# A graph-network kernel's first stage: loading x at once and placing the adjacency check between the layernorms

## The chip, the cores and the metric

The kernel runs on one core of a Trainium2 chip. The metric is the device time of one execution in microseconds (us); a run's time is compared by the median of several executions. The engines are called by the profile's names: PE (TensorE, matrix products), DVE (VectorE), ACT (ScalarE), POOL (GpSimd) and SP (SyncE, which here only issues transfers). A line number such as L391 is a line of the kernel's source; the profile prints it with each instruction.

## The reference, cut to what matters

Four graph layers, each of the form `x = x + layer(relu(layernorm(x)), adj)`, work on x of 8 x 2048 x 64 (batch, node, feature) and one adjacency matrix adj of 2048 x 2048. The first layer is a hypergraph attention, the second a Chebyshev convolution, the third repeats a product with adj three times, the fourth is an attention over neighbours.

```python
def _layernorm(x, axis=-1, eps=1e-5):
    m = jnp.mean(x, axis=axis, keepdims=True)
    v = jnp.var(x, axis=axis, keepdims=True)
    return (x - m) / jnp.sqrt(v + eps)
...
    h = jnp.maximum(_layernorm(x, axis=-1), 0.0)
    x = x + _L0_gnn_ref(h, L0_gnn_H, adj, 64, L0_gnn_W, ...)
...
        h = x @ W          # in _L0_gnn_ref: the "features" of the first layer
        deg = jnp.maximum(adj.sum(-1), 1.0)[:, None]
```

The case is about what the kernel does ahead of the first layer's attention: the first layernorm and relu, the product with W, and a reading of the whole of adj, by which it counts each node's neighbours and decides whether the matrix is sparse enough for its short way.

## The kernel before

**Layout.** x comes transposed, as 4 pairs of batches (`NP`) x 128 (two batches of 64 features, on the partitions) x 2048 nodes. The nodes are worked on in 4 chunks (`NC`) of 512 (`CW`). adj is read in 16 rows of tiles (`NT`), each 128 x 2048, 1 MB; below such a row of tiles is called a row.

**The first stage** is `start` (L629). It loops over the chunks. Each chunk is loaded by `load_x` (L262, into a buffer of two) and normalised by `norm_parts` (L284): for each of the four pairs PE makes a product with `center`, which takes the mean away (L290); ACT squares it (L291); the relu of it goes to `xr`, by turns on DVE (L294) and ACT (L296). PE adds up the squares (`to_rows`), ACT takes the root (L299), DVE its reciprocal (L300). Here the generator yields; `norm` runs it through. The second part spreads the reciprocals over the partitions on PE (`from_rows`) and DVE multiplies (L641), which gives `hn`, kept for the whole first layer in the memory q0 and q1.

`features` (L669) makes, for one chunk, h = hn W in two layouts: four products of 512 columns, copied by ACT to h_t (L676), and four node tiles of sixteen small products, copied by ACT to h_n (L682; memory q4 and q5). In the loop it follows one chunk behind the norms, and for the last chunk it comes after the check.

**The check** is `check_adj` (L368). For each of the 16 rows: SP loads it (L390) into one of four places; ACT squares it, which also adds up the degree (L391); DVE compares the square with the row, to see that all is 0 or 1 (L392); POOL sets the diagonal to zero (L395) and writes the result to `links` in DRAM (L399); PE makes thirteen small products `seen` of it. A place of the four is free for the next load when DVE has compared it, and a place of `squares` when POOL's write and PE's products are done. Then come a few small counts on DVE and PE (L406 to L423) that end in `flag`, a number by which all engines branch into one of two versions of the rest.

**What sets the order.** The tile framework collects the instructions of the program, puts them in an order for each engine by a priority and by its own idea of when each is ready, and adds the waits. An engine then works its instructions in that order and stands still at the first that has to wait. The check is written after the loop over the chunks, and the scheduler itself pulls the rows forward, between the norms. In the order that it builds, ACT squares two rows within and behind chunk 0's norm, then two or four rows at a time; SP issues the first two chunks, the first two rows, and the other two chunks later, when a buffer is free. All PSUM results of norms and features share six banks (`bank`), so a product waits for the reader of the result six places earlier.

`keep_in_program_order` (in `behind`, L193) marks an instruction that the scheduler must keep behind those marked or written ahead of it on its engine. The stage before doesn't use it.

Of the kernel before, what the change touches and what calls it, by code (L numbers as in the profile page):

```python
# [7 lines left out]
F = mybir.dt.float32  # L8
# [4 lines left out]
AF = mybir.ActivationFunctionType  # L13
OP = mybir.AluOpType
# [5 lines left out]
P = 128  # L20
# [3 lines left out]
NP = NB // 2  # L24
NT = N // P
R = P // NP
CW = 512
NC = N // CW
TC = CW // P
# [106 lines left out]
class Kernel:  # L136
# [39 lines left out]
    def mm(self, out, lhsT, rhs, start=True, stop=True):  # L176
        self.nc.tensor.matmul(out, lhsT, rhs, start=start, stop=stop)  # L177
# [102 lines left out]
    def norm(self, *args):  # L280
        for _ in self.norm_parts(*args):
            pass
# [85 lines left out]
    def check_adj(self, pool, slots, seen, ps, flag):  # L368


        nc, adj = self.nc, self.a["adj"]
        limit = self.limits(pool)
        over = pool.tile([P, limit.shape[1] + 2], F, name="over")
        ones = pool.tile([P, P], BF, name="ones")
        nc.vector.memset(ones, 1.0)
        rows = [slots.tile([P, 2, N], F, name=f"rows{i}", tag=f"q{6 + i}") for i in range(2)]
        squares = slots.tile([P, 4, N], BF, name="squares", tag="q8")
        same = pool.tile([P, NT], F, name="same")
        deg = pool.tile([P, NT], F, name="deg")
        own = pool.tile([P, NT], F, name="own")  # L380
        equal = pool.tile([P, N], BF, name="equal")
        one = pool.tile([P, 1], BF, name="one_bf")
        nc.vector.memset(one, 1.0)
        nc.sync.dma_start(
            own, bass.AP(tensor=adj.tensor, offset=adj.offset, ap=[[N + 1, P], [P * (N + 1), NT]])
        )
        for t in range(NT):
            row, sq = rows[t // 2 % 2][:, t % 2], squares[:, t % 4]
            here = slice(t * P, (t + 1) * P)
            nc.sync.dma_start(row, adj[here])  # L390
            nc.scalar.activation(sq, row, AF.Square, accum_out=deg[:, t : t + 1])  # L391
            nc.vector.scalar_tensor_tensor(  # L392
                equal, row, 1.0, sq, op0=OP.mult, op1=OP.is_equal, accum_out=same[:, t : t + 1],
            )
            nc.gpsimd.affine_select(  # L395
                out=sq[:, here], in_=sq[:, here], compare_op=OP.not_equal, fill=0.0, base=0,
                pattern=[[-1, P]], channel_multiplier=1,
            )
            nc.gpsimd.dma_start(self.links[here], sq)  # L399
            for i in range(FAR):  # L400
                c = (HUBS + i) * P
                self.mm(
                    seen[:, t, i : i + 1], sq[:, c : c + P], one,
                    start=t == 0 and i == 0, stop=t == NT - 1 and i == FAR - 1,
                )
        hm = slots.tile([P, NT, D], F, name="hm", tag="q9")  # L406
        nc.sync.dma_start(hm, self.a["H"].rearrange("(t p) e -> p t e", p=P))
        nc.vector.tensor_scalar(hm, hm, 0.0, None, op0=OP.is_gt)
        nc.vector.tensor_reduce(self.deg[:, 0], hm, axis=AX.X, op=OP.add)
        self.count_nodes(pool, ones, limit, over, 0, ps)  # L410
        nc.vector.tensor_sub(self.deg[:, 1], deg, own)
        self.count_nodes(pool, ones, limit, over, 1, ps)
        bad = pool.tile([P, 1], F, name="bad")
        nc.vector.tensor_reduce(bad, same, axis=AX.X, op=OP.add)
        nc.vector.tensor_scalar(over[:, -2:-1], bad, float(N * NT), None, op0=OP.is_lt)
        nc.vector.tensor_scalar(self.edges, seen, 0.0, None, op0=OP.is_gt)
        self.count_lists(pool, ones, limit, over, ps)
        nc.vector.tensor_reduce(bad, over, axis=AX.X, op=OP.max)
        pt = ps.tile([P, CW], F, name="chain")[:1, :P]
        nc.tensor.transpose(pt, bad, self.ident)  # L420
        one = pool.tile([1, 1], F, name="one")
        nc.vector.tensor_reduce(one, pt, axis=AX.X, op=OP.max)
        nc.vector.tensor_scalar(flag, one, 0.0, None, op0=OP.is_gt)  # L423

        nc.vector.memset(self.self_weight, 0.0)
        alone = self.edges.rearrange("p t i -> p (t i)")[:, HUBS * FAR :: FAR + 1]
        weight = self.self_weight[:, HUBS:]
        nc.vector.tensor_scalar(weight, alone, -1.0, 1.0, op0=OP.mult, op1=OP.add)
        nc.vector.tensor_mul(weight, weight, own[:, HUBS:])
        nc.vector.tensor_scalar_max(deg, deg, 1.0)  # L430
        nc.vector.reciprocal(deg, deg)
        pr = ps.tile([P, CW], F, name="chain")[:NT, :P]
        nc.tensor.transpose(pr, deg, self.ident)
        rows = pool.tile([NT, P], F, name="rows")
        nc.vector.tensor_copy(rows, pr)
        nc.sync.dma_start(self.rdeg, rows)
# [192 lines left out]
    def start(self, pool, slots):  # L629

        nc, tc, a = self.nc, self.tc, self.a
        self.deg = pool.tile([P, 2, NT], F, name="deg")
        self.edges = pool.tile([P, NT, FAR], BF, name="edges")
        self.self_weight = pool.tile([P, NT], F, name="self_weight")
        flag = pool.tile([1, 1], I32, name="flag")
        with tc.tile_pool(reuse_waits="tile", name="k00", bufs=1) as k:
            ww = self.block_diag(k, a["W"], "ww")
            hn = Halves(slots, "hn", ("q0", "q1"), False)

            def write(q, ch, xr, scale):  # L640
                nc.vector.tensor_mul(hn(q)[:, ch * CW : (ch + 1) * CW], xr, scale)  # L641

            with (
                tc.tile_pool(reuse_waits="tile", name="links_ps", bufs=1, space=PSUM) as lps,
                tc.tile_pool(reuse_waits="tile", name="ln", bufs=2) as w,
                tc.tile_pool(reuse_waits="tile", name="ln_ps", bufs=6, space=PSUM) as ps,
            ):
                seen = lps.tile([P, NT, FAR], F, name="seen")
                self.h = (
                    hn, Halves(slots, "h_t", ("q2", "q3"), False),  # L650
                    Halves(slots, "h_n", ("q4", "q5"), True),
                )

                def bank():
                    return ps.tile([P, CW], F, name="bank")

                for ch in range(NC):
                    x = self.load_x(w, 0, ch)
                    xr = w.tile([P, NP, CW], F, name="xr", bufs=1)
                    sq = w.tile([P, NP, CW], F, name="sq", bufs=1)  # L660
                    std = w.tile([P, CW], F, name="std", bufs=1)
                    self.norm(ch, x, xr, sq, std, bank, write)
                    if ch > 0:
                        self.features(ww, ch - 1, bank)
                self.check_adj(k, slots, seen, lps, flag)
                self.features(ww, NC - 1, bank)
        return flag

# [2618 lines left out]
```

## Time and profile before

| what | value |
|---|---|
| median of 3 runs (lowest, highest) | 1926.74 us (1921.63, 1930.95) |
| the profiled execution | 1917.82 us |
| its span in the profile | 1916.1 us, 22580 instructions |
| busy shares over the span: PE, DVE, POOL, ACT | 88%, 72%, 56%, 43% |
| flag ready (end of L423) | 96.05 us |
| last copy of the stage's features on ACT (L682) | ends 99.65 us |
| comparisons of rows on DVE (L392), 16 | 36.7 us busy |
| squares of rows on ACT (L391), 16 | 30.4 us busy |
| moved by DMA in the first 97 us | some 30 MB, at about 400 GB/s while it is full |

The busy shares are averages over stages of different kinds, and the chain of waits that the page gives begins only at 809 us, so it says nothing about the first stage. The stage has to be read from its own stretch, 0 to 97 us, which is 5% of the span: from the timeline (start, duration, engine, line, operation, output and input), from the waits of one engine in that stretch, and from a table of busy times by stretches. In such a table each engine's column holds its busy time and, in brackets, the number of its instructions; PEclk is the granted clock of PE as a share of the full one, "DMA share" the mean busy share of the 16 DMA engines.

### The profile page before, as it was taken

The page shows a single profiled execution, that of the slowest core. Times are in us where ns is not written, and L with a number is a line of the kernel's source. Part 1 is how long each engine was busy: PE and PEld are TensorE (multiplying, and loading weights), DVE is VectorE, ACT ScalarE, POOL GpSimd, SP SyncE. Part 2 cuts the span into 40 slices and gives each one's busy share as a digit, 9 for nine tenths or more (in the row PEclk, how much of TensorE's full clock was granted, in tenths as well). Part 3 has the DMA queues.
Part 4 walks back from the last instruction along what each step waited for, and adds up shares of the span by engine and source line. Part 5 has one row for each costly group of instructions (what it writes and reads, how often), then busy time and mean ns, then how long its engine had stood idle before and what let it go on. Part 6 is the DMA issues. An engine that isn't in the chain of part 4 may idle for free.

```text
span 1916.1 us, 22580 instructions
## 1 busy us (share of the span) xinstructions
PE 1682.1 (88%) x7139; PEld 959.6 (50%) x7139; DVE 1376.8 (72%) x2281; ACT 818.7 (43%) x1650; POOL 1078.3 (56%) x1039
## 2 busy tenths in 40 slices
PE   5888899998997788899999999889999999679885
PEld 2446766664333454344343435358777575345432
DVE  6887778884677878778888777557666676558874
ACT  5732544454666654222111010057676754466300
POOL 1101366776762755887687756547373641677760
PEclk8998999998998899999999989999999999789887
DMA  9741223334545774324142232168788774766655
GB/s 340 286 124 46 67 93 101 112 124 159 172 131 152 212 226 155 97 81 125 39 110 98 72 106 77 51 210 274 242 253 261 234 244 148 241 175 180 183 174 196
DMA packets 127372, 305.25 MB, mean 159 GB/s; under 512 B 29681, under 2 KB 33537, under 8 KB 122113
## 3 DMA queue, kind: packets, MB, share of 16 engines
q0 software_dynamic: 45328, 149.60, 26.7%
q1 hardware_dynamic: 79600, 149.82, 23.5%
q10 hardware_dynamic: 2304, 4.20, 0.6%
q8 instruction: 60, 0.98, 0.2%
q14 instruction: 80, 0.65, 0.1%
HBM read 240.41 MB, written 63.14 MB: 158 GB/s over the span
## 4 chain that ended last, share of the span: by engine, by line
PE 35%; DMA 7%; POOL 5%; DVE 5%; issue 4%; ACT 1%; SPq 0%; DVEq 0%; POOLq 0%; ACTq 0%
PE pk L177 17%; PE acc L177 11%; POOL ring L2976 3%; DMA raw<-sent,index 3%; PE bank L177 1%; PE pn L177 1%; DMA ring<-f_rows,near 1%; POOL raw L2646 1%; PE pw L177 1%; PE pz L1955 1%; PE side L177 1%; DMA q<-att_rows 1%; POOL half L1872 1%; PE first L177 1%; PE p L177 1%
## 5 line engine op out<-in xcount | busy, mean ns | idle before, releaser
L2646 POOL DMA_INDIRECT raw<-sent,index x300 | 314.0, 1047 | 286.1 <-DVE part_lo L2664 143.0
L2663 ACT CAST part_hi<-raw 128x512 fp32r<-128x512 f32 x352 | 211.3, 619 | 299.9 <-PE acc L177 202.1
L2664 DVE TENSOR_TENSOR part_lo<-raw,part_hi 128x512 fp32r<-128x512 f32 x352 | 263.6, 769 | 88.4 <-ACT part_hi L2663 80.5
L177 PE MATMUL pk<-q,w 128*128 128x512 f32 (+1 forms) x768 | 305.6, 613 | 5.4 <-DVE q L1753 3.3
L1872 POOL TENSOR_TENSOR half<-half,y 128x512 f32<-128x512 f32 x210 | 263.9, 1287 | 68.5 <-DVE y L1867 67.8
L177 PE MATMUL acc<-q,ident 128*128 128x512 f32 x416 | 202.8, 613 | 23.4 <-DVE q L3066 17.0
L177 PEld LDWEIGHTS pk<-q,w 128*128 128x128 f32 (+1 forms) x768 | 116.1, 190 | 156.8 <-issue 108.7
L177 PE MATMUL acc<-part_lo,weights 128*128 128x512 f32 x365 | 164.5, 452 | 28.4 <-DVE part_lo L2664 28.1
L177 PE MATMUL acc<-part_hi,weights 128*128 128x512 f32 x365 | 171.4, 471 | 19.9 <-ACT part_hi L2663 19.2
L1867 DVE SCALAR_TENSOR_TENSOR y<-pk,bias,q 128x512 f32<-128x512 f32 x210 | 148.2, 744 | 46.6 <-POOL half L1872 23.3
L2976 POOL DMA_INDIRECT ring<-f_rows,near x121 | 140.0, 1157 | 62.8 <-issue 29.2
L177 PEld LDWEIGHTS acc<-q,ident 128*128 128x128 f32 x416 | 76.8, 194 | 97.2 <-issue 42.8
L2355 POOL TENSOR_TENSOR q<-q,beta 128x512 f32<-128x512 f32 x57 | 76.0, 1335 | 71.4 <-DVE beta L2331 32.6
L177 PEld LDWEIGHTS acc<-part_lo,weights 128*128 128x128 f32 x365 | 71.1, 195 | 86.4 <-DVE part_lo L2664 74.0
L177 PEld LDWEIGHTS acc<-part_hi,weights 128*128 128x128 f32 x365 | 70.8, 194 | 69.7 <-ACT part_hi L2663 37.5
L177 PE MATMUL pp<-adj,x_ind_hi 128*128 128x512 f32 x256 | 90.4, 470 | 0.5 <-DVE q L882 0.3
L3047 DVE TENSOR_TENSOR q<-ring,e 128x1024 f32<-128x1024 f32 x58 | 70.1, 1219 | 9.0 <-PE acc L177 8.8
L2632 ACT CAST hub_weights<-dense 128x384 fp32r<-128x384 uint8 x80 | 40.4, 510 | 83.4 <-PE acc L177 83.2
L300 DVE RECIPROCAL std<-std 128x512 f32<-128x512 f32 (+1 forms) x17 | 53.8, 3162 | 30.5 <-ACT std L299 30.5
L2355 POOL TENSOR_TENSOR q<-q,coef 128x512 f32<-128x512 f32 x57 | 63.0, 1106 | 21.0 <-DVE q L2378 17.6
L177 PE MATMUL pp<-adj,x_ind_lo 128*128 128x512 f32 x256 | 72.6, 403 | 0.0
L2563 POOL DMA_INDIRECT listed_raw<-in_adjT_dram,cell x60 | 62.9, 1048 | 16.5 <-issue 15.6
(504 smaller groups left out, 3431.0 us busy)
## 6 DMA issues: line engine op xcount, KB each, us to landing
rows<-in_adj_dram SPq DMA_DIRECT2D x16, 1024.0 KB, 9.5
adj_t<-in_adjT_dram SPq DMA_DIRECT2D x64, 256.0 KB, 3.1
own<-sent SPq DMA_DIRECT2D x52, 256.0 KB, 4.2
raw<-sent SPq DMA_DIRECT2D x52, 256.0 KB, 3.7
sent<-u SPq DMA_DIRECT2D x48, 256.0 KB, 3.2
q<-x SPq DMA_DIRECT2D x9, 1024.0 KB, 5.0
links<-squares POOLq DMA_DIRECT2D x16, 512.0 KB, 8.6
sent<-q SPq DMA_DIRECT2D x32, 256.0 KB, 2.2
```

The costliest lines, as they stand in the source:

```text
L177: self.nc.tensor.matmul(out, lhsT, rhs, start=start, stop=stop)
L300: nc.vector.reciprocal(std, std)
L1867: nc.vector.scalar_tensor_tensor(y, pks[b, half], bias[:, b : b + 1], emb[:, b], op0=OP.add, op1=OP.mult,)
L1872: nc.gpsimd.tensor_add(acc, acc, y)
L2355: self.nc.gpsimd.tensor_tensor(x, x, by.unsqueeze(2).to_broadcast([P, NB, D]), op=OP.mult)
L2563: self.kern.behind(nc.gpsimd.indirect_dma_start(raw[:, i], None, rows, bass.IndirectOffsetOnAxis(ap=self.cell[:, c + i : c + i + 1], axis= ...
L2632: self.nc.scalar.copy(to, self.lists.dense[:, :, i * P : (i + 1) * P])
L2646: self.nc.gpsimd.indirect_dma_start(raw, None, self.rows[:], bass.IndirectOffsetOnAxis(ap=self.lists.index[:, c : c + 1], axis=0),)
L2663: nc.scalar.copy(hi, raw)
L2664: nc.vector.tensor_sub(lo, raw, hi.bitcast(F))
L2976: self.nc.gpsimd.indirect_dma_start(to, None, self.kern.f_rows[:], bass.IndirectOffsetOnAxis(ap=index, axis=0))
L3047: nc.vector.tensor_tensor(y.rearrange("n i (b f) -> n i b f", b=NB), block[:, i : i + 2, : NB * D].rearrange("n i (b f) -> n i b f", b=NB) ...
```

## The change

Three things change in the first stage. All four chunks of x are loaded ahead of everything else; they go into the memory that h_n gets later (chunk 1's place is the first that features overwrites, by then long read). The buffers of x are gone, and `xr` and `std` have two buffers instead of one. The norm of chunk n+1 is done up to its reciprocal before the second part of chunk n is written. And `check_adj` becomes a generator that yields after each row; `start` calls for its rows at fixed places, one or two at a time, and the square on ACT and the comparison on DVE are marked to stay there. The work itself, instruction by instruction, stays the same.

```diff
             nc.sync.dma_start(row, adj[here])
-            nc.scalar.activation(sq, row, AF.Square, accum_out=deg[:, t : t + 1])
-            nc.vector.scalar_tensor_tensor(
-                equal, row, 1.0, sq, op0=OP.mult, op1=OP.is_equal, accum_out=same[:, t : t + 1],
+            self.behind(nc.scalar.activation(sq, row, AF.Square, accum_out=deg[:, t : t + 1]))
+            self.behind(
+                nc.vector.scalar_tensor_tensor(
+                    equal, row, 1.0, sq, op0=OP.mult, op1=OP.is_equal,
+                    accum_out=same[:, t : t + 1],
+                )
             )
...
+            yield
         hm = slots.tile([P, NT, D], F, name="hm", tag="q9")
...
+                h_n = self.h[2].tiles
+                xs = [h_n[c // 2][:, TC * (c % 2) : TC * (c % 2 + 1)] for c in (1, 0, 2, 3)]
                 for ch in range(NC):
-                    x = self.load_x(w, 0, ch)
-                    xr = w.tile([P, NP, CW], F, name="xr", bufs=1)
+                    nc.sync.dma_start(xs[ch], self.xs[0][ch])
+
+                def norm(ch):
+                    xr = w.tile([P, NP, CW], F, name="xr")
                     sq = w.tile([P, NP, CW], F, name="sq", bufs=1)
-                    std = w.tile([P, CW], F, name="std", bufs=1)
-                    self.norm(ch, x, xr, sq, std, bank, write)
+                    std = w.tile([P, CW], F, name="std")
+                    return self.norm_parts(ch, xs[ch], xr, sq, std, bank, write)
+
+                check = self.check_adj(k, slots, seen, lps, flag)
+                norms = [norm(0)]
+
+                def rows(n):
+                    for _ in range(n):
+                        next(check)
+
+                next(norms[0])
+                for ch in range(NC):
+                    if ch + 1 < NC:
+                        norms.append(norm(ch + 1))
+                        next(norms[-1])
+                        rows(2)
+                    for _ in norms[ch]:
+                        pass
+                    rows(1)
                     if ch > 0:
                         self.features(ww, ch - 1, bank)
-                self.check_adj(k, slots, seen, lps, flag)
+                        rows(2)
+                for _ in check:
+                    pass
                 self.features(ww, NC - 1, bank)
```

The write of hn, L641 before, is L645 in the changed source.

## The prediction

> **What bounds the kernel now.** The change touches only the first stage, so I first looked for its end. In the timeline of instructions the flag (L423), by which every engine branches into the rest, ends at 96.05 us of 1916.1. Behind the branch the built orders of both kernels hold the same instructions in the same order on all five engines. What the change is worth is therefore the shift of the flag, and what of this shift the next stage hands on. The table of stretches shows what the stage is made of:
>
> ```profile
> core 0: us, PE busy (x) PEld busy (x) DVE busy (x) ACT busy (x) POOL busy (x), PEclk, DMA share, GB/s
> 5.00:25.00 20.00, 9.34 (x46) 3.54 (x50) 7.41 (x6) 10.22 (x13) 1.02 (x2) 0.84 0.99 361
> 25.00:60.00 35.00, 28.62 (x175) 13.28 (x175) 30.10 (x29) 25.74 (x39) 5.84 (x14) 0.89 1.01 395
> 60.00:65.00 5.00, 5.00 (x15) 1.79 (x8) 5.00 (x7) 4.00 (x6) 0.83 (x2) 0.71 0.84 199
> 65.00:80.00 15.00, 11.55 (x111) 7.23 (x113) 12.87 (x14) 12.48 (x19) 2.88 (x6) 1.00 0.99 382
> 80.00:97.00 17.00, 16.70 (x119) 10.26 (x116) 14.93 (x31) 10.56 (x17) 3.72 (x9) 0.90 0.31 128
> ```
>
> The DMA engines are full until 80 us, but the last 16 us, with a DMA share of 0.31, belong to DVE: the last row is squared by ACT at 81.28, and DVE compares it only at 88.97. DVE never skips work here, so the flag comes at DVE's busy time plus its idle time. Up to 96.1 us it is busy 72.44 us; the idle rest is in the view of waits, for DVE alone (waited for, total, times, longest):
>
> ```profile
> DVE xr L294 <- ACT sq L291: 10.2, 4, 7.1
> DVE equal L392 <- ACT squares L391: 5.2, 3, 3.6
> DVE std L300 <- ACT std L299: 2.8, 3, 1.6
> DVE total L472 <- PE chain L177: 2.4, 2, 2.1
> ```
>
> With 2.7 us of small waits that is 23.3 us. Both kernels give DVE the same instructions, so the flag moves by the change of these 23.3 us. The durations I need stand in the timeline (start, duration):
>
> ```profile
> 21.27 3.35 DVE L300 RECIPROCAL std<-std 128x512 f32<-128x512 f32 x1 [0.87 <-ACT std L299]
> 26.79 2.48 DVE L641 TENSOR_TENSOR q<-xr,bank 128x512 f32<-128x512 f32 x4
> 63.78 2.29 DVE L392 SCALAR_TENSOR_TENSOR equal<-rows,squares 128x2048 bf16<-128x2048 f32 x1
> 61.37 4.42 PE L177 MATMUL bank<-q,ww 128*128 128x512 f32 x8
> 69.40 0.59 ACT L682 COPY q<-bank 128x512 f32<-128x512 f32 x1 [0.31 <-PE bank L177]
> 88.97 2.42 DVE L392 SCALAR_TENSOR_TENSOR equal<-rows,squares 128x2048 bf16<-128x2048 f32 x1
> 95.91 0.14 DVE L423 TENSOR_SCALAR flag<-one 1x1 int32<-1x1 f32 x1
> 99.06 0.59 ACT L682 COPY q<-bank 128x512 f32<-128x512 f32 x1 [0.31 <-PE bank L177]
> ```
>
> From start to start DVE takes 2.29 us for a row's comparison, 3.27 for a reciprocal (21.27 to 24.54), 0.60 for a write of hn or a relu. A group of features, from its first product (61.37) to its last copy (69.99), takes 8.6 us, the next one (81.64 to 90.37) 8.7.
>
> **The change part by part.** *All of x first, two norm halves first: a gain of 1.6 us.* SP issues the four chunks ahead of the rows. Chunk 0 still lands at 8.7 us, with four transfers behind it as before. Until 14.47 DVE does as before. Then ACT has no row's square in its way: last square and relu to 15.3, table load 1.28, root 0.69, and the reciprocal starts at 17.3. So DVE idles 2.9 us where before it idled 3.63 (first comparison) and 0.87 (reciprocal). Two relus and the second reciprocal follow without a wait (ACT needs 3.6 us for chunk 1 meanwhile) until 25.1. Row 0, squared at 16.07 before, has two more chunks of 1.05 MB ahead of it, 2.6 us each at some 400 GB/s: it lands at 21.2, and its square, in ACT's order behind the second root (21.6), ends at 23.5, 1.6 us ahead of DVE. Should the chunks or the small `own` load ahead of it take longer than that, what goes beyond those 1.6 us falls on DVE; SP's queue holds nothing else then.
>
> *The fixed places: a loss of some 3 us.* In the built order ACT now holds each row's square at its place, and the eight copies of a features group stand ahead of rows 6, 11 and 14. I stepped through DVE's and ACT's orders with the durations above. From 25.1 DVE has six comparisons, eight writes, two relus, a reciprocal and the small H step: 13.7 + 4.8 + 1.2 + 3.3 + 0.6, so it is free at 48.7. ACT's root of chunk 2 can't come before 34.4 (its last product waits for a bank that a write at 31.5 frees), and three squares follow: 40.9. Only then can the copies of group 0 run, because products three and four wait for banks that the first copies free. 8.7 us for the group gives 49.7, row 6's square ends at 51.7, DVE starts at 51.8: **3.1 us** idle, where before the same rows cost 0.55 + 1.05. Next: two comparisons, two relus, 57.6; third root 57.9, reciprocal 58.0 (0.4 idle) to 61.3; three comparisons and four writes to 70.6. ACT's squares of rows 8 to 10 end at 63.7 and group 1 at 72.5; the writes of chunk 3 wait for PE, which has these products ahead of theirs, until 72.2 (1.6 idle), and row 11 for its square until 74.5 (1.1 idle). These three replace 0.63, 0.77, 1.62 and 0.27 before. Three comparisons, two writes and 1.5 us on H bring DVE to 84.1. The first count (L472) needs a small product that now stands on PE behind group 2 and two products of group 3: squares to 78.3, group 2 to 85.8 (7.5 us, its first products being done), two products, 87.3: 3.2 us idle, 2.13 before. Row 14's square (87.8) is then ready; its comparison starts at 88.0, the last one at 90.4 and ends at 92.7. From there the tail took 4.65 us before (91.40 to 96.05); with the last features products now ahead of the last row's I add 0.3: flag at **97.6**, 1.5 us later than 96.05.
>
> Stepping through the order of before in the same way gives 95.4, 0.7 early, so the method is good to about 1 us; between the two steps lie 2.2 us, against the time read 1.5. I take 1.5.
>
> *Features behind the flag: worth 0 to 0.9 us.* Before, PE and ACT end group 3 only at 99.65, 3.6 us after the flag; now all of it lies ahead. In the next stage DVE waited 0.90 us for PE once (L518). But its first stop behind that is the load of H's transpose: SP issues it at 99.00, with only two small loads since the flag, and DVE waits 1.62 us for it until 107.33. That load hangs on the flag and not on the features, so I take 0.
>
> *Row loads* are issued when a comparison frees a buffer, as before; four of them stay outstanding, and the DVE idles above all end on ACT or PE, so I cost the loads at nothing beyond row 0. Were that cover gone (a load late by its 9.5 us from issue to landing), the row concerned would cost up to some 5 us. *keep_in_program_order* issues nothing. The writes of links and the `seen` products are the same 16 and 208.
>
> PE's clock enters here. It was granted at 0.50 in 20:27.5 and 80:82.5, after pauses of PE; the first four centre products took 5.13 us, four at full clock 3.60. In my steps PE rests 4 us ahead of the third product of groups 0 and 1, so I paid 1.3 us for two products each time. The Trainium skill (TensorE: Matmul & The Clock Gate, Why this matters for your kernels) warns against this change: a PE idle gap above some 3 us brings half clock, and Part 1 there gives about 3.4 us until it is back. By the page two such gaps would cost, as an estimate, two times 1.7 us and no more; by the trace I have 0.8 each in the group's 8.7.
>
> **The sum.** −1.6 (start) + 3.1 − 1.6 (row 6) + 3.1 − 3.3 (chunk 3, row 11) + 1.1 (count) + 0.3 (tail), that is about +1 in waits, and +1.5 by the steps; the profiled execution, 1917.82 us, becomes 1919.3. That execution is 8.9 us under the median of the runs shown, 1926.74 (1921.63 to 1930.95). On the median's basis I forecast **1928.2 us**.
>
> **The rivals.** *Faster:* the new waits on ACT and PE do not come about, since ACT reaches its copies sooner than I think. Without 3.1 + 0.4 + 1.6 + 1.1 + 1.1 the flag is at 90.3, 5.7 us early: 1921.0. For it: DVE is 1.6 us ahead at 25 us, and the DMA engines could feed it (0.84 in 60:65). Against it: the copies stand ahead of the squares in ACT's order by construction. *Slower:* the features groups run at the pace of the longest one before, 40.26 to 51.57, 11.3 us, because PE starts each cold; all three stand on DVE's path, so 3 x 2.6 us come on top of 1.5: +9.3, 1936.0. It is slower by over 0.5% from groups of 11.4 us on. Against it: that one had a row's square of 1.9 us inside. *No effect:* what is lost in front of the flag is given back behind it, or the order does not become what the text says; the built order shows that it does, and only the 0.9 us above can give anything back: 1926.7.
>
> **How the numbers follow.** Forecast (flag 0 to 4 us late) 0.62, faster rival 0.18, slower rival 0.14, no effect 0.06. Runs of one kernel lie up to 5 us off their median, so the range takes in both rivals with 1 to 2 us beyond: 1919 to 1937. About 0.5% (9.6 us) is what a measurement of this kernel can tell from no change. Faster by more needs the whole stage free of new waits and more: 0.06. Slower by more needs the slower rival with a little besides: 0.11. Within: 0.83.
>
> **What would show it.** In the changed profile the waits of DVE should hold one for row 6's square of 2 to 4 us near 50 us, one of a write (L645) for PE near 72, and the count near 87; the first reciprocals should stand near 17 and 22 us and the flag near 97.6, with no features copies behind it. A flag under 94 with no wait near 50 speaks for the faster rival; groups of features of 11 us and half clock in them for the slower one. I'd be wrong altogether if row loads starved ACT in the middle (waits of L391 on DMA), or if anything behind the flag ran differently.

## The result and the profile after

| | before | changed |
|---|---|---|
| median, 20 runs each (lowest, highest) | 1919.63 us (1911.66, 1930.95) | 1928.97 us (1918.29, 1940.34) |
| the profiled execution | 1917.82 us | 1927.98 us |
| its span | 1916.1 us | 1926.1 us |
| flag ready | 96.05 us | 104.31 us |

The ratio is 1.0044 with a 95% interval of 1.0028 to 1.006, that is 8.4 us (5.4 to 11.5) slower; the two medians themselves lie 9.3 us apart, inside that interval. The median of before is 7.1 us below that of the three runs that the forecast started from. So the time forecast, 1928.2, lies close to the measured 1928.97 by luck, because two differences cancel: the forecast change was +1.5 us, the measured one is +8.4. What has to be explained is the missing 7 us.

The table of stretches of the changed kernel, in places that answer to those of before (each engine's busy time, its instructions in brackets, then PE's granted clock, the DMA share and GB/s):

```profile
core 0: us, PE busy (x) PEld busy (x) DVE busy (x) ACT busy (x) POOL busy (x), PEclk, DMA share, GB/s
5.00:25.00 20.00, 14.76 (x54) 5.24 (x55) 8.56 (x6) 11.88 (x18) 0.00 (x0) 1.00 1.01 362
25.00:60.00 35.00, 27.70 (x159) 12.90 (x158) 29.58 (x31) 23.75 (x35) 7.19 (x16) 0.82 0.96 344
60.00:70.00 10.00, 10.00 (x29) 2.81 (x28) 6.29 (x5) 6.89 (x8) 0.34 (x2) 0.50 0.55 226
70.00:85.00 15.00, 14.77 (x103) 8.38 (x102) 12.42 (x15) 10.33 (x15) 2.98 (x7) 0.85 0.99 345
85.00:105.00 20.00, 15.26 (x133) 11.15 (x129) 12.88 (x30) 11.99 (x19) 5.45 (x8) 1.00 0.42 161
```

The head of the stage is better than before (DVE 8.56 us busy between 5 and 25 us, 7.41 before). Then DVE falls back: in 60:70 it works 6.29 of 10 us, with PE at half its clock, although PE shows no pause in that stretch. The waits of DVE up to 105 us say on whom (waited for, total, times, longest):

```profile
DVE xr L294 <- ACT sq L291: 9.3, 2, 7.1
DVE std L300 <- ACT std L299: 8.2, 4, 4.4
DVE equal L393 <- ACT squares L391: 3.9, 2, 3.7
DVE total L476 <- PE chain L177: 3.7, 1, 3.7
DVE edges L420 <- PE seen L177: 2.4, 1, 2.4
DVE q L645 <- PE bank L177: 2.4, 1, 2.4
```

And the timeline of DVE gives their places (start, duration, ..., idle time before it in brackets):

```profile
17.62 3.35 DVE L300 RECIPROCAL std<-std 128x512 f32<-128x512 f32 x1 [2.65 <-ACT std L299]
...
53.39 2.29 DVE L393 SCALAR_TENSOR_TENSOR equal<-rows,squares 128x2048 bf16<-128x2048 f32 x1 [3.74 <-ACT squares L391]
63.71 3.35 DVE L300 RECIPROCAL std<-std 128x512 f32<-128x512 f32 x1 [4.44 <-ACT std L299]
78.43 1.29 DVE L645 TENSOR_TENSOR q<-xr,bank 128x512 f32<-128x512 f32 x2 [2.40 <-PE bank L177]
93.06 0.39 DVE L476 TENSOR_REDUCE total<-chain 128x14 f32<-128x224 f32 x1 [3.69 <-PE chain L177]
101.43 0.37 DVE L420 TENSOR_SCALAR edges<-seen 128x208 bf16<-128x208 f32 x1 [2.44 <-PE seen L177]
...
104.17 0.14 DVE L427 TENSOR_SCALAR flag<-one 1x1 int32<-1x1 f32 x1
```

Row 6's comparison waits 3.74 us where 3.1 were forecast. Two waits are far larger than forecast: the third root (so the forecast calls the root of chunk 3; chunk 2's is its second) with 4.44 against 0.4, and, at the end, `edges` for the last `seen` product (2.44). Of the 10.2 us between the two profiled executions 8.26 lie ahead of the flag.

### The profile page after: what moved, and what is told of

Same layout as the page of the kernel before. It is cut to its first block, busy times and chain, and to the rows that moved or that the text cites. A ratio compares the mean times of both kernels' runs of the same rounds, so it can differ in the third digit from the quotient of the medians.

```text
span 1926.1 us, 22565 instructions
## 1 busy us (share of the span) xinstructions
PE 1698.4 (88%) x7139; PEld 965.4 (50%) x7139; DVE 1377.6 (72%) x2281; ACT 818.5 (42%) x1650; POOL 1078.7 (56%) x1039
## 5 line engine op out<-in xcount | busy, mean ns | idle before, releaser
L177 PE MATMUL acc<-part_hi,weights 128*128 128x512 f32 x365 | 172.2, 472 | 20.9 <-ACT part_hi L2690 20.0
```

## The experiments

**My theory:** the flag comes late by new waits of DVE, made by the fixed places on ACT and PE, and the delay is handed on whole. **Rivals:** the early loads themselves cost; a low clock of PE alone is it; the delay of the flag is hidden, and the loss sits elsewhere. Times of each group of runs are compared with runs of before on the same chip; two of the three chips were slower as a whole (before at 1983.58 and 1978.23 us).

**A second look at both kernels, unedited.** One profile shows one execution, so I took another of each.

> The kernel before once more, for a second look at its first stage: which of VectorE's waits repeat, and how far the flag moves from one execution to the next with the order of the instructions the same. If the built order sets the waits: flag within 1 of 96.1, the clock's dips at the same places (20 to 30, 60 to 65 and 80 to 85 us). If the granted clock wanders from execution to execution: flag 94 to 99, dips elsewhere.

> The changed kernel once more. A run of the changed kernel with another tail (same order on every engine up to the last features group) had the third root's wait at 1.8 us where the changed kernel's own profile had 4.4, with the clock at 1.00 and not at 0.50 between 60 and 65 us. Theory (order sets row 6's, the scales' and the tail's waits, the clock sets the third root's and the count's size): row 6's wait 3.5 to 4, scales 2 to 4, seen 2 to 2.6 as before; third root anywhere from 1.7 to 4.5, count 0.4 to 3.7; flag 98 to 105. Rival (all of it is set by the order): third root 4.2 to 4.6, count 3.5 to 3.9, flag 104 to 105. Time 1.002 to 1.007 of before in both.

The time ratio came out the same: 1.0044 (1.0027 to 1.006; before 1918.61). The flag was ready at 98.92 us in before and 101.82 in the changed kernel. The order alone does not fix it: it moves by 2.5 to 2.9 us between two executions of one program. DVE's waits in the second look at the changed kernel:

```profile
DVE xr L294 <- ACT sq L291: 9.1, 2, 7.1
DVE std L300 <- ACT std L299: 5.5, 4, 2.7
DVE equal L393 <- ACT squares L391: 3.9, 2, 3.8
DVE edges L420 <- PE seen L177: 3.9, 1, 3.9
DVE q L645 <- PE bank L177: 2.9, 1, 2.9
DVE total L476 <- PE chain L177: 2.0, 1, 2.0
```

Row 6's wait is the same to 0.1 us; the roots, the count and `edges` changed by 1.4 to 2.7. In before, the clock dips lay at the same places again (20 to 30, 60 to 65, 80 to 85 us) but were longer. Where DVE waits repeats, then, and how long moves with the clock. The expectation missed `edges`, which was to stay at 2 to 2.6 us: in the second look the twenty features products ahead of it ran at half clock (PE's timeline, first and then second look):

```profile
98.88 2.48 PE L177 MATMUL bank<-ww,q 128*128 128x128 f32 x20
```

```profile
94.97 3.90 PE L177 MATMUL bank<-ww,q 128*128 128x128 f32 x20
```

The two second looks also speak against the rival of a low clock alone. From 15 to 95 us PE's mean granted clock was 0.91 in the changed kernel and 0.81 in before (0.83 and 0.87 in the first looks), and the changed kernel's flag was still the later one. The mean shift of the flag over both pairs is 5.6 us (8.26 and 2.90).

**Is a late flag handed on?** Before, with DVE work put just ahead of the flag:

```diff
         nc.vector.tensor_reduce(bad, over, axis=AX.X, op=OP.max)
+        slow = pool.tile([P, CW], F, name="slow")
+        nc.vector.tensor_scalar(slow, bad.to_broadcast([P, CW]), 1.0, None, op0=OP.add)
+        for _ in range(6):
+            nc.vector.reciprocal(slow, slow)
+        nc.vector.tensor_scalar(bad, slow[:, :1], 1.5, None, op0=OP.is_gt)
```

> The kernel before with six dependent reciprocals of 128x512 (3.35 us each) and two small operations in VectorE's chain just ahead of the flag, between the largest of over and the transpose: 20.1 + 0.8 us. Theory (a later flag is handed on whole): flag 116.5 to 118, time +19 to +23 against before (1.0096 to 1.0118). Rival (transfers or other engines of the next stage hide a part): +5 to +15.

DVE's timeline shows the delay as meant:

```profile
97.77 20.29 DVE L422 RECIPROCAL slow<-slow 128x512 f32<-128x512 f32 x6
...
119.12 0.14 DVE L428 TENSOR_SCALAR flag<-one 1x1 int32<-1x1 f32 x1
```

Ratio 1.0088 (1.0062 to 1.0114), that is +16.9 us (11.9 to 21.9) for 20.9 us of work. The whole 20.9 lies in the interval, half of it doesn't: the flag is handed on in the main.

**The loads alone.** Before, with x loaded first into h_n's memory, norms whole, nothing put in place:

```diff
...
+                for ch in range(NC):
+                    nc.sync.dma_start(xs[ch], self.xs[0][ch])
                 for ch in range(NC):
-                    x = self.load_x(w, 0, ch)
...
-                    self.norm(ch, x, xr, sq, std, bank, write)
+                    self.norm(ch, xs[ch], xr, sq, std, bank, write)
```

> Only the loads: x is loaded first into h_n's memory as in the change, but each layernorm stays whole and nothing of the check is put in place (it is traced after the loop, as before). Theory (the +8.3 us at the flag are VectorE's waits in the fixed places): no loss from the loads, the first reciprocal near 17.6 us as in the changed kernel, flag 95 to 97, time within 2 us of before. Rival A (the loads themselves cost, since adj's rows come 5 us later and SP's queue is fuller): flag 100 to 104, time +4 to +8 against before.

```profile
17.28 3.35 DVE L300 RECIPROCAL std<-std 128x512 f32<-128x512 f32 x1 [2.53 <-ACT std L299]
...
98.49 0.14 DVE L423 TENSOR_SCALAR flag<-one 1x1 int32<-1x1 f32 x1
```

The first reciprocal comes at 17.28 us as forecast, the flag at 98.63, later than the 95 to 97 expected but within the two looks at before; 1.0007 (0.998 to 1.0033). The early loads are not the loss. Nor are they a gain: in the order that the scheduler then makes, other waits of DVE take it up, as 2.2 us for the scales, which waited for nothing in before.

**The other way round: fixed places, x loaded as before.** The changed kernel with

```diff
...
-                for ch in range(NC):
-                    nc.sync.dma_start(xs[ch], self.xs[0][ch])
...
                 def norm(ch):
+                    x = self.load_x(w, 0, ch)
...
-                    return self.norm_parts(ch, xs[ch], xr, sq, std, bank, write)
+                    return self.norm_parts(ch, x, xr, sq, std, bank, write)
```

> The changed kernel's fixed places with x loaded as before, each chunk into the two x buffers when its norm starts. The forecast counted 1.6 us of gain for loading all of x first. Theory (the gain is that norm 1 has its x at once, which two buffers give as well): first reciprocals within 0.5 of 17.5 and 22.2, flag and time within 2 of the changed kernel. Rival (the two later chunks now stand among adj's rows on SyncE's queue, and their norms or the rows wait): row 6 or the roots of chunks 2 and 3 wait 1 to 4 longer, flag 103 to 107.

The first reciprocals stand at 16.78 and 21.48 us, so two buffers serve the start as well as four early loads; row 6 waits 3.92, the third root 1.80, the scales of chunk 3 4.25, and the flag comes at 102.86, between the two looks at the changed kernel. So far the theory. But its time is 1.010 (1.0064 to 1.0136), 20 us over before, and its profiled execution, 1983.98 us, is the lowest of its seven runs. What the other six lose is in no trace; it stays open.

**Without the marks.** The changed kernel with

```diff
-            self.behind(nc.scalar.activation(sq, row, AF.Square, accum_out=deg[:, t : t + 1]))
-            self.behind(
-                nc.vector.scalar_tensor_tensor(
+            nc.scalar.activation(sq, row, AF.Square, accum_out=deg[:, t : t + 1])
+            nc.vector.scalar_tensor_tensor(
...
```

> The changed kernel without the two marks that keep a row's square and its comparison in traced order; norms in two parts, early x and the yields stay. VectorE's built order is nearly the changed kernel's; ScalarE's order lets squares in between the features copies. Theory: the waits of VectorE for squares behind a group of copies (3.7 at row 6) go, and the wait for the third root (4.4) may stay, since on TensorE the four products from_rows still stand among to_rows: flag 99 to 101, time +3 to +5 against before. Rival B (the marks are all of it): flag 96, time within 1.5 of before. Rival C (early x and norms in two parts are it): flag 104, +8.

```profile
39.88 3.35 DVE L300 RECIPROCAL std<-std 128x512 f32<-128x512 f32 x1 [1.78 <-ACT std L299]
53.32 0.69 DVE L294 TENSOR_SCALAR xr<-bank 128x512 f32<-128x512 f32 x1 [3.33 <-ACT sq L291]
...
96.71 0.14 DVE L424 TENSOR_SCALAR flag<-one 1x1 int32<-1x1 f32 x1
```

By the flag (96.85) rival B wins: without the marks the stage is as short as before in this execution, though its waits are other ones. The time, 1.0029 (0.9997 to 1.0062), decides between nothing and +5 only poorly.

**The third root.** The products of `from_rows` queued behind the next chunk's last `to_rows` on PE:

```diff
+            with self.tc.issue_after(self.root.ins):   # last product of to_rows traced
-            self.from_pair_rows(pr, q, std)
+                self.from_pair_rows(pr, q, std)
```

> The changed kernel with the products of from_rows of a chunk queued on TensorE behind the last to_rows product of the next chunk, so that no chunk's scales stand ahead of the next chunk's variance. In the changed kernel one from_rows product (2.07 us at half the clock) stands between the to_rows products of chunk 3. Theory: VectorE's wait for the third root falls from 4.4 to 2.0 to 2.6, the flag comes 1.5 to 2.5 earlier (102 to 103), time 1.5 to 2.5 below the changed kernel. Rival D (the third root is late for another reason, the low clock or the square's end): wait 4 to 4.8, time unchanged within 1.

```profile
58.88 3.35 DVE L301 RECIPROCAL std<-std 128x512 f32<-128x512 f32 x1 [0.27 <-ACT std L300]
...
75.05 1.29 DVE L647 TENSOR_TENSOR q<-xr,bank 128x512 f32<-128x512 f32 x2 [3.85 <-PE bank L177]
```

The wait falls to 0.27 us, 1.5 below the second look and 4.2 below the first, so the products in between are one cause. What is in between costs 1.12 us at full clock and 2.07 at half. PE's timeline of the two looks at the changed kernel, first look:

```profile
57.20 1.86 PE L177 MATMUL bank<-sq,to_rows 128*32 128x512 f32 x2
58.99 2.07 PE L177 MATMUL bank<-std,from_rows 32*128 32x512 f32 x2
60.99 1.92 PE L177 MATMUL bank<-sq,to_rows 128*32 128x512 f32 x4
```

and second look:

```profile
57.05 1.04 PE L177 MATMUL bank<-sq,to_rows 128*32 128x512 f32 x2
58.02 1.12 PE L177 MATMUL bank<-std,from_rows 32*128 32x512 f32 x2
59.08 1.05 PE L177 MATMUL bank<-sq,to_rows 128*32 128x512 f32 x4
```

The same order, 5.7 us against 3.1 for these products: this is the difference of the third root's wait (4.44 against 1.80). In the edited kernel the scales of chunk 3 took about 1 us of the gain back (3.85 against 2.90). Its flag came at 99.28 us, earlier than the 102 to 103 expected and 2.5 us ahead of the second look: 1.5 of that at the roots, 1.5 at `edges`, whose products ran at full clock, less the 1 us of the scales. Its time, 1.0039 (1.0014 to 1.0063), that is 7.7 us over before, was measured on another chip than the changed kernel's and does not tell a gain of 2 us; it is more than a flag at 99.28 explains.

**The tail.** The last features group queued on PE behind the check's last count:

```diff
-                self.features(ww, NC - 1, bank)
+                with tc.issue_after(self.counted.ins):   # product of count_lists
+                    self.features(ww, NC - 1, bank)
```

> The changed kernel with the products of the last features group queued on TensorE behind the check's last count, so that they no longer stand ahead of the last row's marks of seen. Theory: the waits of VectorE for seen (2.44) and in part for the count ahead of it (3.69) go, the flag comes 2 to 4 us earlier (100 to 102); the features' 8 copies on ScalarE then end behind the flag, and of the 2 to 4 us at least half is lost again there: time 0 to 2 below the changed kernel. Rival E (what stands ahead of seen is only the GpSimd chain): flag 104, time +2 to +5, since features then end 4 us behind the flag.

The count's wait fell to 0.35 us and that of `edges` to 0.99, but the chain of the flag met the features all the same, on PE at half clock, ahead of the transpose of `bad` (L425):

```profile
97.57 3.66 PE L177 MATMUL bank<-q,ww 128*128 128x512 f32 x4
101.03 0.42 PE L425 MATMUL chain<-ident,bad 128*1 128x128 f32 x1
```

Flag 101.95, and ACT copies until 107.7 instead of 102.0 and reads the flag only at 107.2, 5.2 us late. Time 1.0068 (1.0039 to 1.0097), 13.5 us over before. The forecast's "features behind the flag worth 0 to 0.9" has a place where it does not hold: pushed behind the flag as a whole, they hold up ACT, whose first work in the next stage starts 8.5 us behind the flag, against 5.3 in the changed kernel.

**Rows ahead of the features groups.** In the loop of `start`, the two rows that follow a group put ahead of it:

```diff
-                    rows(1)
+                    rows(3 if ch > 0 else 1)
                     if ch > 0:
                         self.features(ww, ch - 1, bank)
-                        rows(2)
```

> The changed kernel with the two rows that follow a features group put ahead of it (three rows after each norm, none behind the group), so that no square stands behind a whole group of copies on ScalarE. Theory: row 6's wait (3.7 us) falls below 0.7, flag 2 to 4 earlier than the changed kernel in the same call, time 2 to 4 below it. Rival (the wait moves on: group 0's copies end later and with them the squares of chunk 3 on ScalarE): row 6 below 0.7, but xr of chunk 3 and the third root wait as much, flag unchanged within 1.

```profile
DVE xr L294 <- ACT sq L291: 11.1, 3, 7.3
DVE std L300 <- ACT std L299: 5.9, 4, 2.5
DVE edges L420 <- PE seen L177: 1.1, 1, 1.1
DVE q L645 <- PE bank L177: 1.0, 1, 1.0
DVE equal L393 <- ACT squares L391: 1.0, 1, 1.0
```

Flag 94.73, 7.1 us below the second look at the changed kernel; time 1.0007 (0.999 to 1.0025) against 1.0044 (1.0027 to 1.006) for the changed kernel on the same chip. The intervals don't meet: this order gives back 7 us of the 8.4. Row 6's wait is gone, `xr` of chunk 3 waits 1.95 more, and the scales, the count and `edges` fall from 8.8 together to 2.7. It is more than the 2 to 4 us expected. POOL's long step of row 14 (last section), which lies ahead of `edges` in both looks at the changed kernel, is absent in this run and in the two that follow, and no run separates its 2 us from the rest. To see which place does it, the same edit at one place each:

```diff
-                    rows(1)
+                    rows(3 if ch == 1 else 1)        # the other run: ch == NC - 1
                     if ch > 0:
                         self.features(ww, ch - 1, bank)
-                        rows(2)
+                        rows(0 if ch == 1 else 2)
```

> The rows-ahead order at the first features group alone (rows 6 and 7 ahead of group 0); the two rows behind groups 1 and 2 stay there. In the run with all rows ahead the flag came 7.1 us earlier than in the changed kernel's second look (94.8 against 101.9), and VectorE's waits fell at row 6 (3.8 to 0), at the scales of chunk 3 (2.9 to 1.0), at the first count (2.0 to 0.7) and at seen (3.9 to 1.1), while xr and the third root of chunk 3 rose by 2.4 together. Theory (each place pays for itself): row 6's wait goes, xr and the third root give 1 to 2.4 of it back, the scales, the count and seen stay as in the changed kernel: flag 98 to 101, time +3 to +7 against before. Rival (row 6 is the head of all the later waits): flag 94 to 96, time within 2 of before.

> The rows-ahead order at the last of the three groups alone (the two rows that follow group 2 are put ahead of it); row 6 stays behind group 0. Theory (each place pays for itself): row 6's wait 3.7 stays, the count's and seen's waits fall from 5.9 to 1 to 2.5 together: flag 97 to 100, time +2 to +6 against before. Rival (row 6 is the head of all the later waits): count and seen stay at 5 to 6, flag 101 to 104, time +7 to +9.

Row 6 alone: flag 94.91, as with all three; no wait at `edges` and none at the count. The last group alone: flag 101.0, row 6 waits 3.72, the count 1.52, `edges` 0.64, and a comparison late in the stage 1.66. By the flags the rival wins, that the place of row 6 decides the later waits too. But its own sign fails in the second run: the count and `edges` were to keep 5 to 6 us between them and kept 2.2, while other waits grew. Nor is the first edit clean, for the scheduler still places the small counts itself, and with row 6 moved it put the first count behind row 14's comparison, where nothing waits for it. The times, 1.003 (1.0004 to 1.0055) and 1.004 (1.001 to 1.007), on one of the slower chips, don't separate the two.

**All that helped, and an earlier start.** Rows ahead and the root first, W's two loads behind those of x, chunk 0 in four parts:

```diff
-            ww = self.block_diag(k, a["W"], "ww")
...
-                for ch in range(NC):
+                for q in range(NP):
+                    nc.sync.dma_start(xs[0][:, q], self.xs[0][0][:, q])
+                for ch in range(1, NC):
                     nc.sync.dma_start(xs[ch], self.xs[0][ch])
+                ww = self.block_diag(k, a["W"], "ww")
```

> All rows ahead of the groups, from_rows behind the next chunk's to_rows on TensorE, and the loads of x put ahead of W's two on SyncE's queue, chunk 0 in four parts (SyncE spends 1.23 us on W's two issues ahead of x, and the first product waits for all of chunk 0 until 8.7 us). Theory (a flag is handed on whole, and DVE's waits are what is left of it): the start comes 1 to 2.5 us earlier, the third root's wait falls from 2.2 to 0.3 to 1, the scales of chunk 3 may take 1 of it back: flag 90.5 to 93.5, time 3 to 7 below before (0.9963 to 0.9985). Rival (what is won at the head is lost to the row loads or to a colder TensorE): flag 94 to 96, time within 2 of before.

```profile
14.22 3.35 DVE L301 RECIPROCAL std<-std 128x512 f32<-128x512 f32 x1 [2.66 <-ACT std L300]
...
53.66 0.69 DVE L294 TENSOR_SCALAR xr<-bank 128x512 f32<-128x512 f32 x1 [5.90 <-ACT sq L291]
```

The first reciprocal comes 3.2 us earlier than in the run before (17.40), and the `xr` of chunk 3 still at 53.66 us, where that run had 53.67: DVE waits 5.90 there instead of 1.95. ACT's waits show a part of what lies between: those for a row's load and for the writes of links have grown from 0.2 and 2.5 us to these:

```profile
ACT squares L393 <- DMA links<-squares: 4.1, 3, 1.7
ACT squares L393 <- DMA rows<-in_adj_dram: 1.8, 2, 1.4
```

ACT's root of chunk 2 comes 4.4 us earlier than in the run before. From there to the `xr` of chunk 3 ACT waits 1.65 us for a write of links and 1.25 for nothing that the profile names; the rest of the 4.4 goes on PE, whose clock was granted at 0.63 between 40 and 50 us, against 0.83 in the run before. Flag 94.5, time 1.0018 (0.9987 to 1.0049). The rival was right: what is won at the head is lost to the transfers and to a lower clock. No version beat before; the best equals it.

## Why the prediction was wrong in size

The mechanism is the forecast one: the start gains, the fixed places lose, the flag is late and is handed on. The size is not. The forecast's steps, with its idle times and those of the two looks at the changed kernel (us):

| step | forecast | first look | second look |
|---|---|---|---|
| all of x first: first comparison starts | 25.1 | 25.59 | 25.43 |
| second root (chunk 2) | 0 | 0.88 | 0.88 |
| row 6 | 3.1 | 3.74 | 3.76 |
| third root | 0.4 | 4.44 | 1.80 |
| scales of chunk 3 (the write) | 1.6 | 2.40 | 2.90 |
| row 11 | 1.1 | 0.18 | 0.18 |
| first count | 3.2 | 3.69 | 2.04 |
| tail, end of the last comparison to flag | 4.65 + 0.3 | 6.00 | 7.45 |
| flag | 97.6 | 104.31 | 101.82 |

The differences add up to 7.5 and 5.0 us, the flags differ by 6.7 and 4.2; the 0.8 left over in both is, by difference, work that my steps counted too long.

- **All of x first:** right to 0.5 us.
- **Row 6, the largest single forecast:** right in place and mechanism, 0.65 too small. With row 6 ahead of its group the flag came 7 us earlier, more than its own wait, but other places moved with it; what is row 6's alone isn't shown.
- **Third root, 0.4:** the term that failed. I stepped through ACT's and DVE's orders and took PE as ready there. The built order has products of `from_rows` among those of `to_rows`, which cost 1.5 us (the edit that puts them behind left 0.27), and a half clock, in the first look, 2.6 more.
- **Scales 1.6:** right in place and in cause (PE works on group 1 first), 0.8 to 1.3 too small.
- **Second root, 0:** 0.88 too small in both looks, by a half clock (0.50 from 30 to 35 us): its last centre product took 2.07 us, the one before it 1.12. From the write that frees the bank to the root the forecast had 2.9 us, the first look 4.7 (31.3 to 36.0).
- **Tail, 0.3:** the other term that failed, 1.1 and 2.5 too small. The forecast saw features products ahead of the last `seen`, but not that POOL's step ahead of them would take 2.4 us, so that twenty products come to lie on the path (see the last section); in the second look these ran 1.4 us longer, at half clock.
- **Count, row 11:** within 1.2; the count once above and once below the forecast, row 11 0.9 below.
- **Row loads at nothing:** right in the changed kernel (no wait of a square for DMA there), but no longer so in the order with rows ahead (2.7 us of such waits) and with an earlier start (5.9).
- **Handed on whole:** not refuted (16.9 us of 20.9, with 20.9 inside). *Features behind the flag, 0:* right for this change. Matched instruction by instruction, DVE's work 20 to 60 us behind the flag comes 0.5 and 0.9 us sooner after it than in before.
- **PE's clock:** the forecast read two drops in before, at 20:27.5 and 80:82.5. The trace has two more, at 37.5:42.5 (0.79, then 0.52) and 60:62.5 (0.50). The changed kernel has four between 25 and 85 us in the first look and three in the second.
- **The rivals:** the faster one failed at once, its waits came. The slower one, groups of features started cold by PE's pauses, did not come as written: groups took 9.2, 8.7 and 8.1 us, from the first copy's start to the last one's end, where the forecast had 8.7. Yet the time is near its +9.3; the low clock hit elsewhere, at the third root.

**Open.** Over both pairs the profiled executions differ by 10.2 and 5.3 us, their flags by 8.3 and 2.9. So some 2 us in each lie behind the flag, where DVE's starts, matched instruction by instruction, wander from place to place: by -4 to +2 us between the kernels, by -3 to +5.5 between two executions of one kernel. Whether these 2 us belong to the change isn't settled. Of the runs on the slower chips no profile of before exists, and their flags explain their times poorly: those at 94.5, 94.9 and 99.3 took 3.6, 5.9 and 7.7 us more than before. The excess has one sign. Against the mean flag of the two looks at before (97.5), the changed kernel took 2.8 us more than its flag says, and the eight kernels built from it 4 to 14 more, on all three chips; of the two built from before, the loads alone took 0.3 more and the delay 4.9 less. So it seems that something comes with the change besides the late flag; no run shows what.

## What to carry to other kernels

When work is pinned in an order, step through all the engines in the built order, PE and POOL too, and price what stands in front of each instruction that the bounding engine waits for; the two terms that I took over as small were the two where I had not done so. Take a second profile before explaining waits of one to three microseconds: here one program's flag moved by 2.5 to 2.9 us between executions. And don't queue a row's work behind a whole group of copies: here, putting two rows ahead of each group gave back 7 us.

## What the runs showed of the hardware

**POOL and DVE lock each other out, and 0.05 us decide who pays.** The step on the diagonal (L395 before, L398 now, 128x128, on POOL) takes 0.28 us nearly always. For row 14 it is released, in both kernels, just as DVE goes on to the last comparison. POOL's timeline of before:

```profile
88.96 0.28 POOL L395 TENSOR_SCALAR_AFFINE_SELECT squares<-squares 128x128 bf16<-128x128 bf16 x1 [1.39 <-DVE deg L411]
```

DVE's comparison began at 88.97, 0.01 later, and took 2.42 us in place of 2.28. POOL's timeline of the changed kernel:

```profile
96.07 2.39 POOL L398 TENSOR_SCALAR_AFFINE_SELECT squares<-squares 128x128 bf16<-128x128 bf16 x1 [6.99 <-DVE deg L415]
```

Here the comparison (2.29 us) had begun at 96.02, 0.05 earlier; POOL's step ends 0.15 after it. So who starts second waits: 0.14 us for DVE, 2.1 for POOL. PE's timeline of the changed kernel shows what the 2.1 cost: the last marks of row 14 wait, twenty features products come behind them, and the last mark of row 15 behind these.

```profile
98.52 0.50 PE L177 MATMUL seen<-one_bf,squares 128*128 128x1 bf16 x14 [2.07 <-POOL squares L398]
98.88 2.48 PE L177 MATMUL bank<-ww,q 128*128 128x128 f32 x20
101.20 0.17 PE L177 MATMUL seen<-one_bf,squares 128*128 128x1 bf16 x1
```

The fourteen profiles agree. In five (both looks at the changed kernel, x late, root first, tail) POOL starts 0.05 to 0.06 us behind the comparison and takes 2.39 or 2.40; in three (both looks at before, and with the delay) it starts 0.01 ahead and takes 0.28, the comparison 2.42; in the other six the step of row 14 takes 0.28 to 0.32. No run varied this by itself, nor is it shown why POOL starts 0.06 us later in the one family. The Trainium skill ("SBUF — State Buffer", section "SBUF: two separate sides") states the rule: DVE and GpSimd share a pair of ports as an exclusive lock, held for the whole instruction by the one that starts first, among DVE's operations also by those with two SBUF inputs, against a GpSimd operation that reads SBUF. The rows agree with it.

**Half clock without a long pause.** In the first look PE's clock was granted at 0.50 from 57.3 to 70.9 us, after a pause of 1.2 us (54.6 to 55.8), and PE was busy in every microsecond of those 13.6. In the second look the same pause brought no drop, and a later one of some 2.4 us brought 3.4 us at half clock. What decides between the two, no run shows. The forecast had cited the Trainium skill (TensorE: Matmul & The Clock Gate, Why this matters for your kernels, and Part 1) for pauses above some 3 us and about 3.4 us until the clock is back; the rows of the first look show a shorter pause and four times that, and they decide.
